# Two heads' scores in neighbouring PSUM banks, and one exponential for both, in a two-layer cross-attention kernel

## The chip, the cores and the metric

The kernel runs as one program on one core of one Trainium2 chip. Its work is spread over five engines: TensorE (PE in the profile, with PEld for its weight loads), VectorE (DVE), ScalarE (ACT), GpSimd (POOL) and SyncE (SP), which issues nearly all DMAs. The metric is the device time of one execution in microseconds, as a median over runs.

## The reference

Two layers, each of a self-attention, a cross-attention and a gated feed-forward part, on four sequences of 512 tokens of width 320, with a context of 1601 tokens of width 192 for each sequence. There are 20 heads of width 16. Everything is float32.

```python
def _attn(x, ctx, wq, wk, wv, wo, bo, heads):
    q, k, v = heads_of(x @ wq), heads_of(ctx @ wk), heads_of(ctx @ wv)
    sim = einsum('bhid,bhjd->bhij', q, k) * dh ** (-0.5)
    out = einsum('bhij,bhjd->bhid', softmax(sim), v)
    return out.transpose(0, 2, 1, 3).reshape(b, n, heads * dh) @ wo + bo

h1 = _ln(x, n1_g, n1_b);  x = _attn(h1, h1, q1, k1, v1, o1_w, o1_b, heads) + x
h2 = _ln(x, n2_g, n2_b);  x = _attn(h2, context, q2, k2, v2, o2_w, o2_b, heads) + x
h3 = _ln(x, n3_g, n3_b);  a, g = split(h3 @ ff_w1 + ff_b1, 2)
x = a * gelu(g) @ ff_w2 + ff_b2 + x
```

(The two layers' code is the same; `heads_of` stands for the reshape and transpose into heads.)

## The kernel before

The work is cut into units. A unit is one layer, one kind (self or cross), one sequence and one group of four heads; a feed-forward unit is one sequence of one layer. There are 20 self units and 20 cross units in each layer. The keys of a unit go in chunks of 128: four chunks in a self unit, 13 in a cross unit (the last has 65 keys), so 680 chunks in all.

For each chunk, `score` makes the scores of one head, transposed (keys on partitions, 512 queries in the columns), in one PSUM bank called "st", by three products of 32 rows each: two for query parts `q` (a value is split into a high and a low part) and one that adds the negative row maximum `nrows`. `exponential` then reads the bank with one ACTIVATE (line 1290) into an SBUF buffer "pr". There are four such buffers to a chunk, one for each head.

Beside the scores of a unit, the row maxima of a later one are made: `max_pairs` (line 1040) makes scores in the other orientation, in banks called "sps", and DVE reduces each bank to a maximum (line 1069), into `pm` for a cross unit and into `nmax` for a self unit. Four heads sit in four row groups of PE, so that a product of each runs at the same time. `round_of` (line 1243) lays the products of a chunk out in slots: heads 0 and 1 of the scores in slots 0 to 2 with "sps" of heads 2 and 3 in slots 0 and 1, then heads 2 and 3 of the scores in slots 2 to 4 with "sps" of heads 0 and 1 in slots 3 and 4. A full chunk thus uses four "st" and four "sps" banks, which are all eight of PSUM.

After the slots of a chunk come the products with the values for the chunk before (`values`, line 1299, put off through `late` and `flush`): eight matmuls into one bank "av", for which a bank must be free. For chunk 0 the bank is copied to `o`; for later ones ACT copies it to a buffer "vo" (line 1325) and POOL adds that to `o` (line 1326). In the last unit ahead of a feed-forward part DVE adds straight from the bank. Then `steps` (line 473) puts in small pieces of other units' work: the projections "qkps" and "qps", the context's keys "kps" (line 951), values "vps" (line 1015), the output projection "ops" (line 1209), and the DMAs that go with them.

The order on every engine is the order in which the program emits the work. Which bank a product gets is decided as the program is written, by a planner: `expect` holds the time at which the program believes each engine to be free, `written` and `busy` move it on by a booked cost, and `bank` gives the bank that will be free first. The same times decide, in `taken` (line 991), whether DVE or ACT copies a small product out of PSUM. Each of the eight banks is a pool slot of its own, and the chip's waits follow from which bank was given.

The buffers "pr", "vo", "gl" (the gate of the feed-forward part, line 1462) and the warm-up operand "fill" come in turn from one pool of nine buffers of 512 columns.

Of the kernel before, what the change touches and what calls it, by code (L numbers as in the profile page):

```python
# [75 lines left out]
def kernel(ctx: ExitStack, tc: tile.TileContext, x, context, ws, out):  # L76
# [27 lines left out]
    prs = ctx.enter_context(tc.tile_pool(name="prs", bufs=9))  # L104
# [27 lines left out]
    fill = prs.tile([P, N], F32, tag="pr", name="fill")  # L132
# [264 lines left out]
    bank_of = {}  # L397

    def bank(name):
        i = min(range(NB), key=lambda i: bank_free[i])  # L400
        assert bank_free[i] < HELD, name
        t = psum.tile([P, 512], F32, tag=f"bank{i}", name=name)
        bank_of[id(t)] = [i, t, bank_free[i], 0.0]
        bank_free[i] = HELD
        return t
# [6 lines left out]
    def busy(engine, us, *tiles):  # L412
        expect[engine] = max([expect[engine]] + [bank_of[id(t)][3] + 0.05 for t in tiles]) + us
        for t in tiles:
            bank_free[bank_of[id(t)][0]] = expect[engine] + 0.09
# [854 lines left out]
    def main(u, give, nxt):  # L1270

        pr, raised = {}, {}

        def score(c, j):
            r = min(P, u.nkeys - c * P)
            rows = slice(j * SLOT, (j + 1) * SLOT)
            own = []

            def product(e):
                nc.tensor.matmul(  # L1280
                    own[0][:r, :],
                    lhsT=ones[rows, :r] if e == 2 else u.keys(rows, c),
                    rhs=u.rows[rows, :] if e == 2 else u.q[rows, e, :],
                    start=(e == 0),
                    stop=(e == 2),
                )

            def exponential():
                p = prs.tile([P, N], F32, tag="pr", name="pr")
                nc.scalar.activation(p[:r], own[0][:r], AF.Exp)  # L1290
                pr[c, j] = p
                busy("act", 0.515, *own)
                raised[c] = expect["act"]

            return (j,), [lambda e=e: product(e) for e in range(3)], exponential, own, lambda: own.append(bank("st"))
# [3 lines left out]
        def values(c):  # L1299
# [18 lines left out]
            if c == 0:  # L1318
                u.o = two.tile([P, N], F32, tag="o", name="o")
                (nc.vector.tensor_copy if last else nc.scalar.copy)(u.o, ps)  # L1320
            elif last:
                nc.vector.tensor_tensor(u.o, ps, u.o, ALU.add)
            else:
                vo = prs.tile([P, N], F32, tag="pr", name="vo")
                nc.scalar.copy(vo, ps)  # L1325
                nc.gpsimd.tensor_tensor(u.o, u.o, vo, ALU.add)  # L1326
# [3 lines left out]
        for c in range(u.nch):  # L1330
            extra = []
            if last:
                round_of([lambda j=j: score(c, j) for j in range(HG)])
                tick()
            else:
                products = []
                for odd in range(2):
                    if odd:
                        tick()
                    pair, rounds = give(2 * c + odd)  # L1340
                    extra += rounds
                    products += [lambda j=j: score(c, j) for j in ((2, 3) if odd else (0, 1))] + pair
                round_of(products)
# [71 lines left out]
    def ff_main(u, give, nxt):  # L1415
# [44 lines left out]
        def gate(c, pss):  # L1460
            gl = prs.tile([P, N], F32, tag="pr", name="gl")
# [5 lines left out]
        def banks():  # L1467
            return [[bank("fps") for _ in range(2)] for _ in range(2)]
# [3 lines left out]
        for j, c in enumerate(ORDER):  # L1472
            ahead = pss is not None
            some = []
            if not ahead:
# [3 lines left out]
                pss = [some, [bank("fps") for _ in range(2)]] if some else banks()  # L1479
# [7 lines left out]
            if not ahead:  # L1487
                rests(c, these, False)
                if j + 1 < len(ORDER):
                    pss = banks()  # L1490
                    rests(ORDER[j + 1], pss, True)
# [237 lines left out]
```

## Time and profile before

| What | Value |
|---|---|
| median of the runs | 3000.01 us |
| lowest and highest of three | 2998.21 and 3005.65 us |
| the profiled execution's own time | 3000.91 us |
| its span, first to last instruction | 2999.1 us |
| TensorE clock granted | 0.993 of full speed |
| exponentials (line 1290) | 2720, of 603 ns in the mean |

The profile names an instruction by its line and by out<-in, with the program's names for tiles. A matmul's end is modelled, so PE's busy share is not a share of its peak. A line of waits says which engine and line waited for which, with the total in microseconds, the number of times and the longest; a wait of PEld is that of a weight load, which stands in front of its matmul. A line of the timeline has the start and length in microseconds, then the instruction, how many of them were merged, and in brackets the engine's idle time before it with what ended it.

The scores of line 1280 run from 44.5 to 2722.2 us, with a pause in the middle (three of 40 equal slices of the span without any) in which the first layer's feed-forward part lies; the second layer's lies behind them.

### The profile page before, as it was taken

The page shows a single profiled execution, that of the slowest core. Times are in us where ns is not written, and L with a number is a line of the kernel's source. Part 1 is how long each engine was busy: PE and PEld are TensorE (multiplying, and loading weights), DVE is VectorE, ACT ScalarE, POOL GpSimd, SP SyncE. Part 2 cuts the span into 40 slices and gives each one's busy share as a digit, 9 for nine tenths or more (in the row PEclk, how much of TensorE's full clock was granted, in tenths as well). Part 3 has the DMA queues.
Part 4 walks back from the last instruction along what each step waited for, and adds up shares of the span by engine and source line. Part 5 has one row for each costly group of instructions (what it writes and reads, how often), then busy time and mean ns, then how long its engine had stood idle before and what let it go on. Part 6 is the DMA issues. An engine that isn't in the chain of part 4 may idle for free.

```text
span 2999.1 us, 84363 instructions
## 1 busy us (share of the span) xinstructions
PE 2885.4 (96%) x35018; PEld 1509.7 (50%) x35018; DVE 2150.8 (72%) x4143; ACT 1892.7 (63%) x3746; POOL 1194.0 (40%) x1305
## 2 busy tenths in 40 slices
PE   8999999999999999999999899999999999999999
PEld 4455554555554554355554555555555555544555
DVE  6877888889889888323268788888888888873221
ACT  3766677877877878501147676778778778784000
POOL 3444344544544545211224443445445454451110
PEclk9999999999999999999999999999999999999999
DMA  4444223132232122200123342222221121222000
GB/s 107 103 122 102 71 74 96 46 90 60 53 82 67 39 56 60 82 17 15 37 60 74 91 99 66 66 58 53 53 64 46 49 70 44 54 54 76 22 22 14
DMA packets 186543, 188.70 MB, mean 63 GB/s; under 512 B 69668, under 2 KB 137264, under 8 KB 186160
## 3 DMA queue, kind: packets, MB, share of 16 engines
q1 hardware_dynamic: 185368, 182.11, 24.0%
q8 instruction: 276, 4.52, 0.6%
q10 hardware_dynamic: 760, 1.18, 0.2%
q14 instruction: 107, 0.88, 0.1%
q0 software_dynamic: 32, 0.00, 0.0%
HBM read 55.76 MB, written 29.36 MB: 28 GB/s over the span
## 4 chain that ended last, share of the span: by engine, by line
PE 77%; DVE 18%; DMA 1%; issue 1%; ACT 1%; POOL 1%; SPq 1%; ACTq 0%; DVEq 0%; POOLq 0%
PE av L1306 21%; PE st L1280 15%; PE fps L1391 9%; DVE pm L1069 9%; PE sps L1054 6%; PE yps L1498 6%; PE vps L1015 4%; DVE nmax L1069 4%; PE ops L1209 3%; PE kps L951 3%; PE qkps L886 3%; PE fps L1451 2%; PE qps L927 2%; PE sps L1081 1%; DVE hturned L608 1%
## 5 line engine op out<-in xcount | busy, mean ns | idle before, releaser
L1290 ACT ACTIVATE pr<-st 128x512 f32<-128x512 f32 (+1 forms) x2720 | 1405.0, 603 | 429.1 <-PE st L1280 381.4
L1069 DVE TENSOR_REDUCE pm<-sps 128x1 f32<-128x512 f32 x1920 | 1185.3, 681 | 129.6 <-PE sps L1054 121.5
L1326 POOL TENSOR_TENSOR o<-o,vo 128x512 f32<-128x512 f32 x576 | 740.7, 1286 | 1125.9 <-ACT vo L1325 1114.3
L1054 PE MATMUL sps<-kT,q 32*128 32x512 f32 x4800 | 874.4, 429 | 13.7 <-DMA q<-low 4.3
L1306 PE MATMUL av<-pr,vals 128*32 128x512 f32 (+1 forms) x5440 | 738.4, 609 | 74.7 <-DVE nmax L1069 19.3
L1280 PE MATMUL st<-q,kT 32*128 32x512 f32 (+1 forms) x5120 | 795.7, 421 | 7.1 <-DVE pm L1069 6.4
L1280 PEld LDWEIGHTS st<-q,kT 32*128 32x128 f32 (+1 forms) x5120 | 422.9, 180 | 299.5 <-issue 120.1
L1280 PE MATMUL st<-nrows,ones 32*128 32x512 f32 (+1 forms) x2720 | 542.6, 399 | 5.4 <-DMA nrows<-turned 5.4
L1054 PEld LDWEIGHTS sps<-kT,q 32*128 32x128 f32 x4800 | 424.0, 183 | 102.2 <-DVE pm L1069 26.8
L1069 DVE TENSOR_REDUCE nmax<-sps 128x1 f32<-128x512 f32 x640 | 395.2, 680 | 81.1 <-PE sps L1054 77.9
L1325 ACT COPY vo<-av 128x512 f32<-128x512 f32 x576 | 352.3, 612 | 26.8 <-PE av L1306 24.7
L1462 ACT ACTIVATE gl<-fps,b 128x512 f32<-128x512 f32 x80 | 54.8, 687 | 414.3 <-PE fps L1451 303.0
L1306 PEld LDWEIGHTS av<-pr,vals 128*32 128x32 f32 (+1 forms) x5440 | 111.1, 108 | 348.8 <-DVE pm L1069 180.7
L1391 PE MATMUL fps<-hT,w 128*128 128x512 f32 x640 | 283.2, 597 | 0.0
L1280 PEld LDWEIGHTS st<-nrows,ones 32*128 32x128 f32 (+1 forms) x2720 | 247.0, 180 | 28.2 <-DMA nrows<-turned 4.8
L1463 DVE SCALAR_TENSOR_TENSOR hid<-fps,b,gl 128x512 f32<-128x512 f32 x80 | 59.7, 748 | 238.8 <-ACT gl L1462 236.7
L1391 PEld LDWEIGHTS fps<-hT,w 128*128 128x128 f32 x640 | 119.2, 190 | 155.1 <-issue 152.6
L1498 PE MATMUL yps<-w,hid 128*128 128x320 f32 x640 | 176.0, 435 | 0.1
L1498 PEld LDWEIGHTS yps<-w,hid 128*128 128x128 f32 x640 | 120.4, 190 | 56.4 <-ACT gl L1462 5.3
L1209 PEld LDWEIGHTS ops<-wo,aT 112*32 112x32 f32 (+1 forms) x3072 | 98.0, 110 | 64.6 <-issue 42.9
L1209 PE MATMUL ops<-wo,aT 112*32 112x160 f32 (+1 forms) x3072 | 126.2, 301 | 0.9 <-DVE pm L1069 0.9
L1505 DVE TENSOR_TENSOR x<-yps,x 128x320 f32<-128x320 f32 x32 | 15.7, 492 | 145.9 <-PE yps L1498 145.9
(89 smaller groups left out, 2476.1 us busy)
## 6 DMA issues: line engine op xcount, KB each, us to landing
kT<-stages SPq DMA_DIRECT2D x160, 200.2 KB
oway<-o SPq DMA_DIRECT2D x80, 256.0 KB
q<-high SPq DMA_DIRECT2D x160, 64.0 KB
q<-low SPq DMA_DIRECT2D x160, 64.0 KB
kT<-high SPq DMA_DIRECT2D x60, 128.0 KB
q<-high SPq DMA_DIRECT2D x60, 128.0 KB
kT<-low SPq DMA_DIRECT2D x57, 128.0 KB
aT<-oway SPq DMA_DIRECT2D x32, 224.0 KB
```

Of the source, the lines that this page charges most:

```text
L886: nc.tensor.matmul(ps[f : f + m, :w], lhsT=wqk[:n, k, f // GD, column : column + m], rhs=first.hT[:n, k, at : at + w], start=(k == 0), sto ...
L1015: nc.tensor.matmul(ps[f : f + m, :w], lhsT=u.kvT[:n, k, at + f : at + f + m], rhs=wv[:n, k, h0 * DH : h1 * DH], start=(k == 0), stop=(k == ...
L1054: nc.tensor.matmul(ps, lhsT=u.q[j * SLOT : (j + 1) * SLOT, e, t * P : (t + 1) * P], rhs=u.kT[j * SLOT : (j + 1) * SLOT, u.k0 + s * 512 : u ...
L1069: nc.vector.tensor_reduce(to[:, j : j + 1], ps, AX.X, ALU.max, negate=(ns == 1))
L1209: nc.tensor.matmul(ps[f : f + m, : D // 2], lhsT=aT[:n, k, f * NQ + t * SLOT : f * NQ + t * SLOT + m], rhs=wo[:n, k, cols], start=(k == 0) ...
L1280: nc.tensor.matmul(own[0][:r, :], lhsT=ones[rows, :r] if e == 2 else u.keys(rows, c), rhs=u.rows[rows, :] if e == 2 else u.q[rows, e, :], ...
L1290: nc.scalar.activation(p[:r], own[0][:r], AF.Exp)
L1306: nc.tensor.matmul(ps[j * SLOT : (j + 1) * SLOT, :], lhsT=columns_of[:r, head : head + SLOT], rhs=pr.pop((c, j))[:r, :], start=True, stop= ...
L1325: nc.scalar.copy(vo, ps)
L1326: nc.gpsimd.tensor_tensor(u.o, u.o, vo, ALU.add)
L1391: nc.tensor.matmul(ps, lhsT=w1[:, k, i * FF + c * P : i * FF + (c + 1) * P], rhs=natural(u.hT[:, k]), start=start, stop=stop,)
L1498: nc.tensor.matmul(ps[:, :D], lhsT=hid[c][:, t * P : (t + 1) * P], rhs=w2[:, c, :], start=(c == 0), stop=(c == NHC - 1),)
```

## The change

`score` now makes the scores of two heads, in two neighbouring banks of which the first has an even number, and one ACTIVATE of 1024 columns reads both into two neighbouring buffers. The order of the products in the slots stays as it was. The eight banks become one PSUM tile of eight slices; `bank` can give two of them at once, and takes for that the even pair whose later one is free first. `busy` marks both banks as read. The planner books 0.88 us for the exponential of two heads, where it booked 0.515 us for one.

The nine buffers become one SBUF tile. Pairs of heads take slices 0 to 7 in turn, two chunks' worth. A "vo" of an odd chunk takes the slice in which head 2 of its own chunk was, which `values` has read by then, and one of an even chunk takes slice 8, as does the warm-up operand. The gate takes all nine in turn. The function `banks` of the feed-forward part is only renamed.

```diff
-    prs = ctx.enter_context(tc.tile_pool(name="prs", bufs=9))
+    prs = ctx.enter_context(tc.tile_pool(name="prs", bufs=1))
...
-    fill = prs.tile([P, N], F32, tag="pr", name="fill")
+    raise_to = prs.tile([P, 9, N], F32, name="pr")
+    raises = {"pair": 0, "sum": 0, "gate": 0}
+
+    def turn_of(what, n):
+        raises[what] += 1
+        return raises[what] % n
+
+    fill = raise_to[:, 8]
...
-    def bank(name):
-        i = min(range(NB), key=lambda i: bank_free[i])
-        assert bank_free[i] < HELD, name
-        t = psum.tile([P, 512], F32, tag=f"bank{i}", name=name)
-        bank_of[id(t)] = [i, t, bank_free[i], 0.0]
-        bank_free[i] = HELD
+    banks = psum.tile([P, NB, 512], F32, name="banks")
+
+    def bank(name, n=1):
+        at = min(range(0, NB - n + 1, n), key=lambda i: max(bank_free[i : i + n]))
+        free = max(bank_free[at : at + n])
+        assert free < HELD, name
+        t = banks[:, at] if n == 1 else banks[:, at : at + n]
+        bank_of[id(t)] = [range(at, at + n), t, free, 0.0]
+        for i in range(at, at + n):
+            bank_free[i] = HELD
         return t
...
         for t in tiles:
-            bank_free[bank_of[id(t)][0]] = expect[engine] + 0.09
+            for i in bank_of[id(t)][0]:
+                bank_free[i] = expect[engine] + 0.09
...
-        def score(c, j):
+        def score(c, heads):
             r = min(P, u.nkeys - c * P)
-            rows = slice(j * SLOT, (j + 1) * SLOT)
             own = []
 
             def product(e):
-                nc.tensor.matmul(
-                    own[0][:r, :],
...
+                for i, j in enumerate(heads):
+                    rows = slice(j * SLOT, (j + 1) * SLOT)
+                    nc.tensor.matmul(
+                        own[0][:r, i],
...
             def exponential():
-                p = prs.tile([P, N], F32, tag="pr", name="pr")
+                at = 2 * turn_of("pair", 4)
+                p = raise_to[:, at : at + 2]
                 nc.scalar.activation(p[:r], own[0][:r], AF.Exp)
-                pr[c, j] = p
-                busy("act", 0.515, *own)
+                for i, j in enumerate(heads):
+                    pr[c, j] = p[:, i]
+                summing[c] = p[:, 0]
+                busy("act", 0.88, *own)
                 raised[c] = expect["act"]
 
-            return (j,), [lambda e=e: product(e) for e in range(3)], exponential, own, lambda: own.append(bank("st"))
+            return heads, [lambda e=e: product(e) for e in range(3)], exponential, own, lambda: own.append(bank("st", 2))
...
-                vo = prs.tile([P, N], F32, tag="pr", name="vo")
+                vo = summing.pop(c) if c % 2 else raise_to[:, 8]
...
-                round_of([lambda j=j: score(c, j) for j in range(HG)])
+                round_of([lambda j=j: score(c, (j, j + 1)) for j in range(0, HG, 2)])
...
-                    products += [lambda j=j: score(c, j) for j in ((2, 3) if odd else (0, 1))] + pair
+                    products += [lambda j=2 * odd: score(c, (j, j + 1))] + pair
...
-            gl = prs.tile([P, N], F32, tag="pr", name="gl")
+            gl = raise_to[:, turn_of("gate", 9)]
```

More of the change, by code (lines that the diff above doesn't have):

```diff
@@ L1465, in gate, with four @@
             busy("dve", 0.66, pss[0])
-        def banks():
+        def four():
             return [[bank("fps") for _ in range(2)] for _ in range(2)]
@@ L1478, in ff_main @@
                 begun.clear()
-                pss = [some, [bank("fps") for _ in range(2)]] if some else banks()
+                pss = [some, [bank("fps") for _ in range(2)]] if some else four()
             for e in range(2):
@@ L1489, in ff_main @@
                 if j + 1 < len(ORDER):
-                    pss = banks()
+                    pss = four()
                     rests(ORDER[j + 1], pss, True)
```

12 lines of the change are left out of this document (6 added, 6 removed).

## The prediction

> **What bounds the kernel now.** I read the page first (busy shares, the chain that ended last), then the groups by line, then the waits, and last the timeline of one chunk of a cross unit.
>
> ```profile
> span 2999.1 us, 84363 instructions
> PE 2885.4 (96%) x35018; PEld 1509.7 (50%) x35018; DVE 2150.8 (72%) x4143; ACT 1892.7 (63%) x3746; POOL 1194.0 (40%) x1305
> PE 77%; DVE 18%; DMA 1%; issue 1%; ACT 1%; POOL 1%; SPq 1%; ACTq 0%; DVEq 0%; POOLq 0%
> PE av L1306 21%; PE st L1280 15%; PE fps L1391 9%; DVE pm L1069 9%; PE sps L1054 6%; PE yps L1498 6%; PE vps L1015 4%; DVE nmax L1069 4%; PE ops L1209 3%; PE kps L951 3%; PE qkps L886 3%; PE fps L1451 2%; PE qps L927 2%; PE sps L1081 1%; DVE hturned L608 1%
> ```
>
> PE is busy for 96% of the span and carries 77% of the chain. DVE carries 18%, and 9% and 4% of that are the row maxima of line 1069. ACT, whose instructions the change merges, is 63% busy and has 1% of the chain. So ACT's throughput is not what is short. The waits say what PE lacks:
>
> ```profile
> ACT pr L1290 <- PE st L1280: 381.4, 510, 23.2
> PEld av L1306 <- DVE pm L1069: 180.7, 354, 1.6
> PEld st L1280 <- ACT pr L1290: 97.5, 134, 0.8
> PEld av L1306 <- ACT pr L1290: 79.1, 160, 0.7
> PEld av L1306 <- DVE nmax L1069: 68.7, 103, 4.7
> PE av L1306 <- DVE nmax L1069: 19.3, 13, 4.2
> ```
>
> The product "av" does not read the maxima of line 1069. It waits for them because it needs a PSUM bank: four score banks and four "sps" banks are all eight, and whichever is read out first is av's. That is a reduction 354 + 103 times and an exponential 160 times. ACT itself waits for PE for 381.4 us, so it has idle time to spare. One chunk:
>
> ```profile
> 803.20 0.49 PE L1280 MATMUL st<-q,kT 32*128 32x512 f32 x2
> ...
> 803.54 0.40 PE L1054 MATMUL sps<-kT,q 32*128 32x512 f32 x2
> ...
> 803.98 2.48 DVE L1069 TENSOR_REDUCE pm<-sps 128x1 f32<-128x512 f32 x4 [0.27 <-PE sps L1054]
> ...
> 804.19 2.06 ACT L1290 ACTIVATE pr<-st 128x512 f32<-128x512 f32 x4 [0.86 <-PE st L1280]
> ...
> 804.24 0.39 PE L1280 MATMUL st<-nrows,ones 32*128 32x512 f32 x2
> ...
> 804.72 0.16 PEld L1306 LDWEIGHTS av<-pr,vals 128*32 128x32 f32 x8 [0.52 <-DVE pm L1069]
> 804.73 1.06 PE L1306 MATMUL av<-pr,vals 128*32 128x512 f32 x8
> ...
> 806.12 0.62 ACT L1325 COPY vo<-av 128x512 f32<-128x512 f32 x1
> 806.40 0.49 PE L1280 MATMUL st<-q,kT 32*128 32x512 f32 x2
> ...
> 806.97 0.39 PE L1280 MATMUL st<-nrows,ones 32*128 32x512 f32 x2
> 806.98 0.40 PE L1280 MATMUL st<-q,kT 32*128 32x512 f32 x2
> ```
>
> The first reduction starts at 803.98, as soon as its scores are there, and with it av's bank comes free; the weights of av start at 804.72. The four exponentials run from 804.19 to 806.25. The chunk starts at 803.20 and the next at 806.40, and its second pair of scores (heads 2 and 3) at 806.98.
>
> **The change, part by part.**
>
> ```profile
> L1290 ACT ACTIVATE pr<-st 128x512 f32<-128x512 f32 x2560 | 1323.3, 603 | 403.8 <-PE st L1280 367.6 <-PE sps L1081 27.2 <-PE sps L1054 4.5
> L1325 ACT COPY vo<-av 128x512 f32<-128x512 f32 x576 | 352.3, 612 | 26.8 <-PE av L1306 24.7 <-POOL root L521 0.6
> L997 ACT COPY vals<-vps 128x192 f32<-128x192 f32 x48 | 15.7, 328 | 20.8 <-PE vps L1015 20.2
> L935 ACT ACTIVATE low<-qps 128x256 f32<-128x256 f32 x40 | 15.4, 385 | 23.9 <-PE qps L927 23.9
> L1290 ACT ACTIVATE pr<-st 65x512 f32<-65x512 f32 x160 | 82.0, 594 | 25.3 <-PE st L1280 13.8 <-PE sps L1054 11.3
> L1069 DVE TENSOR_REDUCE pm<-sps 128x1 f32<-128x512 f32 x1920 | 1185.3, 681 | 129.6 <-PE sps L1054 121.5 <-PE st L1280 3.5
> ```
>
> *The exponential.* 2560 + 160 instructions of 512 columns become 1360 of 1024. No row shows 1024 columns. From 256 to 512 columns an ACTIVATE goes from 385 to 603 ns, 0.85 ns a column; copies of 192 and 512 columns give 0.89. So 512 more columns cost 436 ns (to 454), and the long one takes 1.04 us. Four exponentials took 2.06 us in the chunk, so they start (2.06 - 0.60) / 3 = 0.49 us apart; two of 1024 start 0.49 + 0.43 = 0.92 apart. A pair saves 2 x 0.49 - 0.92 = 0.05 us, about 70 us of ACT over 1360. I cost this gain at nothing: ACT's 381.4 us of waiting for PE cover it.
>
> *When banks come free.* In the chunk shown, the first score bank is free at 804.19 + 0.60 = 804.79 now and the other three by 806.25. After the change the first two are free together at 805.23 and the last two at 806.15: the first bank comes 0.44 us later, the last 0.10 earlier. Where a reduction gives av its bank, nothing moves: it ends about 804.67, ahead of both. Where an exponential does (160 waits), av waits longer, by 0.44 us at most and by nothing where a reduction ends just then. The rows do not say which; I take half, 0.22 x 160 = +35 us (ends 0 and 70).
> The Trainium skill speaks against the change here: Perfetto Trace Analysis, section Optimizing Scalar/DVE Operations, says that where Scalar or Vector is not saturated but causes bubbles on other engines, breaking instructions up may let work finish sooner. This trace agrees as far as ACT at 63% ends 160 waits of av; by that rule taken in full the term is its upper end, 70 in place of 35, and the sum is 35 us higher.
>
> *Two neighbouring banks.* A pair of scores now needs an even bank and the next one both free, while sps, av and the copied products take the single bank that is free first and so break pairs. By hand from the chunk: av takes the bank of the first reduction, the next small product one of heads 0 and 1; the next chunk's first pair takes two banks free by 806.15, and its second pair is left with av's bank and that of the last reduction. The last reduction ends at 803.98 + 2.48 = 806.46, the copy of av, which starts 0.11 before the exponential ahead of it ends (0.60 - 0.49), at 806.15 - 0.11 + 0.61 = 806.65. The pair is wanted at 806.98, so 0.33 us is spare, and the steady chunk loses nothing. Chunks where scores wait for exponentials already (134 waits) can lose up to 0.44 each: 0 to 59 us; I take a quarter, +15, since the chunk shown has slack.
>
> *The buffer of vo.* In odd chunks vo now lies in the buffer of heads 2 and 3 of its own chunk, which the second exponential of the chunk after next writes again; before, the buffer came back one chunk later.
>
> ```profile
> L1326 POOL TENSOR_TENSOR o<-o,vo 128x512 f32<-128x512 f32 x576 | 740.7, 1286 | 1125.9 <-ACT vo L1325 1114.3 <-DMA w<-in_L_xattn_ff_w_dram 4.0 <-DMA nrows<-turned 2.7
> L804 POOL TENSOR_TENSOR stages<-stages 128x801 f32<-128x801 f32 x40 | 64.1, 1603 | 3.2
> L803 POOL CAST stages<-stages 128x801 fp32r<-128x801 f32 x40 | 34.2, 856 | 43.3 <-ACT stages L997 16.6 <-DVE stages L994 10.9 <-DVE pm L1069 8.7
> ```
>
> POOL's addition would end at 806.65 + 1.29 = 807.94, and that exponential starts one chunk (803.20 to 806.40, 3.20 us) after 805.11, at 808.31: 0.37 us spare. The 40 splits of 0.86 + 1.60 us on POOL's queue can push an addition past that, in half the chunks: 20 x (2.46 - 0.37) = 42 us of late exponentials at most. Behind a waiting exponential stand the vo copy and ACT's evictions, and behind those PE's banks; ACT's idle time takes most of it. +5 us.
>
> *Copies that change engine.* The planner gives a small copy to the engine it believes free first, and it now books 0.88 us a pair in place of 1.03, so some go from DVE to ACT.
>
> ```profile
> L994 DVE COPY vals<-vps 128x192 f32<-128x192 f32 (+3 forms) x167 | 53.3, 320 | 39.2 <-PE vps L1015 33.6 <-POOL o L1326 1.7
> L994 DVE COPY stages<-kps 128x200 f32<-128x200 f32 (+1 forms) x120 | 44.2, 369 | 40.8 <-PE kps L951 25.9 <-ACT vo L1325 4.0 <-issue 3.1
> ```
>
> DVE does 287 of them, 98 us. Fewer can only help where DVE is behind. The waits for pm are 180.7 / 354 = 0.51 us, the 0.52 of the chunk shown, whose reduction began at once, so there is no backlog to win. The waits for nmax are 68.7 / 103 = 0.67, so 0.15 x 103 + 19.3 = 35 us is the most. I take -10 (ends -35 and 0).
>
> The slices that stand for tiles (first warm-up operand, gate buffers) add no work.
>
> **Sum.** 35 + 15 + 5 - 10 = +45 us (ends -35 and +171). The profiled execution took 3000.91 us, 1.8 more than its span; 3046 by it, and 3045 by the median of the runs, 3000.01, which is 0.9 below it. The runs lie within 0.25% of each other, so about 0.3% (9 us) is what can be told from no change.
>
> **The rivals.**
> *Faster:* ACT's room takes the copies off DVE, and the planner, which books the score banks later, hands av a reduction's bank each time. The wait is av behind nmax and the 160 behind exponentials lose nothing: -35 us, less the 5 for vo, 2970. For it: DVE's 18% of the chain. Against: the pm waits hold no backlog. It decides where the 160 waits cost under 0.1 us each. 0.22.
> *Nothing measurable:* a reduction frees av's bank in nearly all chunks and the slack of 0.33 us holds for the pairs: 3000. For it: 457 of the 617 waits of av. 0.10.
> *Broken pairs cost every chunk:* the second pair waits for the last reduction or the copy of av. It begins when DVE is over 0.5 us late or ACT 0.33. At 0.25 us over the 520 chunks of the cross units (two layers of 20 units of 13) it is +130, 3131. For it: DVE at 72% over all, with copies ahead of reductions. Against: the slack. 0.14.
> *Shared tiles are waited for whole,* so that the change does not do what it says: av waits for the latest exponential, 806.15 in place of 804.67, 1.48 us in 680 chunks (1360 pairs), about 4000 us. Against it:
>
> ```profile
>   DVE pm L1069: 190.7, 367
>   ACT pr L1290: 95.1, 230
>   DVE nmax L1069: 88.0, 116
>   issue: 12.5, 32
>   DVE pm L1091: 2.5, 7
>   DVE turned L1123: 1.4, 3
>   DVE parts L1119: 0.4, 1
> ```
>
> This is all that av's line waits for, and the copies into "vals", one tile that av reads while later chunks are copied into it, are not there. But no PSUM tile is shared yet. 0.04.
>
> **How the numbers follow.** The forecast, slower by 45 us, has 0.50, its own range 3015 to 3085. With the rivals: slower 0.50 + 0.14 + 0.04 = 0.68, same 0.10, faster 0.22. The range for 8 in 10 takes in most of the faster case and the lower half of the broken pairs: 2970 to 3115.
>
> **What would show it.** Exponentials: 1360 of about 1.04 us, some 70 us less ACT busy. The waits of av for pr: fewer or as many, but longer on the mean than 0.49 us. The waits of st for pr or for pm: longer. Copies of line 994: fewer than 287. POOL as a releaser of the exponentials: new, a few us. The prediction is wrong if av's waits for pr all but vanish while those for pm stay, or if PE waits for pairs in most chunks.

## The result and the profile after

The changed kernel takes 3027.37 us in the median (3027.20 to 3030.76), the kernel before 3001.51 over the runs made beside it: a ratio of 1.0088, with a 95% interval from 1.0075 to 1.0101. It is slower by 26 us, on the side that was forecast and inside the range, at about 0.6 of the 45 us. The profiled execution of after took 3027.30 us, its span is 3025.5, and its granted clock is 0.993, as in before.

In after every PSUM tile is called "banks" and every exponential's buffer "pr", so its products must be told apart by line: 1292 makes the scores for the exponentials ("st" before), 1065 and 1092 those for the maxima ("sps"), 1321 is the product with the values ("av"), 1080 the reductions, 1303 the exponential, 1340 the copy of av and 1341 the addition on POOL.

The page of after, busy shares and the chain by engine:

```profile
span 3025.5 us, 84304 instructions
PE 2875.7 (95%) x35018; PEld 1518.0 (50%) x35018; DVE 2157.9 (71%) x4153; ACT 1825.6 (60%) x2376; POOL 1194.1 (39%) x1305
...
PE 76%; DVE 17%; issue 2%; ACT 2%; POOL 1%; DMA 1%; SPq 1%; DVEq 0%; POOLq 0%; ACTq 0%
```

ACT is busy for 67.1 us less (1892.7 before) and the kernel is slower all the same. ACT's share of the chain has gone from 1% to 2%. The groups that carry the change, from the page of after (the last number of the middle part is the mean time of one in ns):

```profile
L1303 ACT ACTIVATE pr<-banks 128x1024 f32<-128x1024 f32 (+1 forms) x1360 | 1329.7, 1022 | 460.5 <-PE banks L1292 395.3
...
L1292 PEld LDWEIGHTS banks<-q,kT 32*128 32x128 f32 (+1 forms) x5120 | 434.3, 180 | 315.5 <-ACT pr L1303 131.9
...
L1321 PEld LDWEIGHTS banks<-pr,vals 128*32 128x32 f32 (+1 forms) x5440 | 108.1, 108 | 392.1 <-DVE pm L1080 227.7
```

and the two lines of weight loads that answer to them, from the page of before:

```profile
L1280 PEld LDWEIGHTS st<-q,kT 32*128 32x128 f32 (+1 forms) x5120 | 422.9, 180 | 299.5 <-issue 120.1
...
L1306 PEld LDWEIGHTS av<-pr,vals 128*32 128x32 f32 (+1 forms) x5440 | 111.1, 108 | 348.8 <-DVE pm L1069 180.7
```

The weight loads of av stand idle 43.3 us longer, those of the scores 16.0 longer. A wait of a weight load can lie beside matmuls that still run, so these are no losses as they stand; the starts of the matmuls, below, say what was lost. The releasers, some rows from the waits of after:

```profile
ACT pr L1303 <- PE banks L1292: 395.3, 566, 4.9
PEld banks L1321 <- DVE pm L1080: 227.7, 409, 1.6
PEld banks L1292 <- ACT pr L1303: 133.8, 212, 1.7
PEld banks L1321 <- DVE nmax L1080: 92.0, 130, 3.8
PEld banks L1321 <- ACT pr L1303: 45.2, 50, 1.1
PE banks L1321 <- DVE pm L1080: 38.8, 102, 1.2
PE banks L1321 <- DVE nmax L1080: 33.9, 51, 3.4
ACT pr L1303 <- POOL o L1341: 15.0, 51, 0.7
```

Av was released by an exponential 160 times and is now 50 times, at 45.2 / 50 = 0.90 us each where it was 0.49. A reduction releases it oftener (409 + 130 against 354 + 103 times), and that is where the waiting grew: for pm from 180.7 to 227.7 us and for nmax from 68.7 to 92.0, while the waits for exponentials fell from 79.1 to 45.2. One and the same chunk, where both changes are seen, first in the timeline of before:

```profile
685.91 2.06 ACT L1290 ACTIVATE pr<-st 128x512 f32<-128x512 f32 x4 [0.66 <-PE st L1280]
...
685.96 0.39 PE L1280 MATMUL st<-nrows,ones 32*128 32x512 f32 x2
...
686.56 1.07 PE L1306 MATMUL av<-pr,vals 128*32 128x512 f32 x8 [0.21 <-ACT pr L1290]
...
687.03 2.44 DVE L1069 TENSOR_REDUCE pm<-sps 128x1 f32<-128x512 f32 x4
687.73 0.50 PEld L951 LDWEIGHTS kps<-ctxT,w 96*32 96x32 f32 x16 [1.02 <-DVE pm L1069]
687.73 0.89 PE L951 MATMUL kps<-ctxT,w 96*32 96x200 f32 x16
...
688.55 0.45 PE L1280 MATMUL st<-q,kT 32*65 32x512 f32 x2
```

and then in that of after:

```profile
695.75 1.94 ACT L1303 ACTIVATE pr<-banks 128x1024 f32<-128x1024 f32 x2 [0.78 <-PE banks L1292]
...
695.78 0.39 PE L1065 MATMUL banks<-kT,q 32*128 32x512 f32 x1
...
696.81 2.44 DVE L1080 TENSOR_REDUCE pm<-banks 128x1 f32<-128x512 f32 x4
...
696.83 1.07 PE L1321 MATMUL banks<-pr,vals 128*32 128x512 f32 x8 [0.65 <-ACT pr L1303]
...
697.71 0.86 PE L962 MATMUL banks<-ctxT,w 96*32 96x200 f32 x16
...
698.50 0.44 PE L1292 MATMUL banks<-q,kT 32*65 32x512 f32 x2
```

Before, an exponential of 0.60 us that began at 685.91 let av start at 686.56; the product after it then waited for a reduction and started 1.17 us after av. After, the exponential that began at 695.75 lets av start at 696.83, 1.08 us behind it in place of 0.65; the product after it finds its bank free and starts 0.88 us after av. Most of what av loses here, the next product gives back: from the exponential's start to that product it is 687.73 - 685.91 = 1.82 us before and 697.71 - 695.75 = 1.96 after.

To see this for the whole span, I added up the time from the start of each matmul to the start of the next, over all of PE's matmuls of a profiled execution, and sorted it into four: from a score product to a score product right behind it; from a chunk's last score product to av; from av's first product until the first product behind av; and everything else. A score product is here one of either kind, for the exponentials or for the maxima.

| us of the profiled span | among the scores | scores to av | av to the next | other | span |
|---|---|---|---|---|---|
| before | 856.1 | 318.0 | 649.4 | 1170.2 | 2999.1 |
| after | 857.3 | 363.0 | 630.0 | 1170.0 | 3025.5 |
| difference | +1.2 | +45.0 | -19.4 | -0.2 | +26.4 |

(The span also holds 5.3 us ahead of the first matmul and behind the last one's start, the same in both.) So the whole loss lies ahead of av, 45 us, and 19 of it come back behind av. The experiments show that the +1.2 among the scores is not "nothing", but a sum of larger terms of opposite signs.

### The profile page after: what moved, and what is told of

The parts are those of the page before. It is cut to its first block, busy times and chain, and to the rows that moved or that the text cites. A ratio compares the mean times of both kernels' runs of the same rounds, so it can differ in the third digit from the quotient of the medians.

```text
span 3025.5 us, 84304 instructions
## 1 busy us (share of the span) xinstructions
PE 2875.7 (95%) x35018; PEld 1518.0 (50%) x35018; DVE 2157.9 (71%) x4153; ACT 1825.6 (60%) x2376; POOL 1194.1 (39%) x1305
## 4 chain that ended last, share of the span: by engine, by line
PE 76%; DVE 17%; issue 2%; ACT 2%; POOL 1%; DMA 1%; SPq 1%; DVEq 0%; POOLq 0%; ACTq 0%
PE banks L1321 21%; PE banks L1292 15%; DVE pm L1080 10%; PE banks L1406 9%; PE banks L1513 6%; PE banks L1065 5%; PE banks L1026 5%; PE banks L1220 3%; DVE nmax L1080 3%; PE banks L962 3%; PE banks L897 3%; PE banks L1466 2%; PE banks L938 2%; ACT pr L1303 2%; PE banks L1092 1%
## 5 line engine op out<-in xcount | busy, mean ns | idle before, releaser
L1303 ACT ACTIVATE pr<-banks 128x1024 f32<-128x1024 f32 (+1 forms) x1360 | 1329.7, 1022 | 460.5 <-PE banks L1292 395.3
L1080 DVE TENSOR_REDUCE pm<-banks 128x1 f32<-128x512 f32 x1920 | 1187.5, 682 | 132.0 <-PE banks L1065 122.6
L1341 POOL TENSOR_TENSOR o<-o,pr 128x512 f32<-128x512 f32 x576 | 741.4, 1287 | 1151.2 <-ACT pr L1340 1124.6
L1065 PE MATMUL banks<-kT,q 32*128 32x512 f32 x4800 | 862.4, 428 | 11.2 <-DMA q<-high 3.0
L1321 PE MATMUL banks<-pr,vals 128*32 128x512 f32 (+1 forms) x5440 | 732.6, 608 | 116.9 <-DVE pm L1080 38.8
L1292 PE MATMUL banks<-q,kT 32*128 32x512 f32 (+1 forms) x5120 | 816.1, 422 | 10.7 <-DVE pm L1080 2.9
L1292 PEld LDWEIGHTS banks<-q,kT 32*128 32x128 f32 (+1 forms) x5120 | 434.3, 180 | 315.5 <-ACT pr L1303 131.9
L1292 PE MATMUL banks<-nrows,ones 32*128 32x512 f32 (+1 forms) x2720 | 556.7, 395 | 1.2 <-DMA nrows<-turned 1.2
L1065 PEld LDWEIGHTS banks<-kT,q 32*128 32x128 f32 x4800 | 427.2, 183 | 78.8 <-ACT pr L1303 17.2
L1080 DVE TENSOR_REDUCE nmax<-banks 128x1 f32<-128x512 f32 x640 | 396.2, 681 | 81.9 <-PE banks L1065 79.4
L1321 PEld LDWEIGHTS banks<-pr,vals 128*32 128x32 f32 (+1 forms) x5440 | 108.1, 108 | 392.1 <-DVE pm L1080 227.7
```

Of the source, the lines that this page charges most:

```text
L1065: nc.tensor.matmul(ps, lhsT=u.q[j * SLOT : (j + 1) * SLOT, e, t * P : (t + 1) * P], rhs=u.kT[j * SLOT : (j + 1) * SLOT, u.k0 + s * 512 : u ...
L1080: nc.vector.tensor_reduce(to[:, j : j + 1], ps, AX.X, ALU.max, negate=(ns == 1))
L1292: nc.tensor.matmul(own[0][:r, i], lhsT=ones[rows, :r] if e == 2 else u.keys(rows, c), rhs=u.rows[rows, :] if e == 2 else u.q[rows, e, :], ...
L1321: nc.tensor.matmul(ps[j * SLOT : (j + 1) * SLOT, :], lhsT=columns_of[:r, head : head + SLOT], rhs=pr.pop((c, j))[:r, :], start=True, stop= ...
```

## The experiments

One execution can lie 8 us off its kernel's median: of the kernel below that splits only the first pair, the profiled one took 3026.60 us at a granted clock of 0.990, and two at 0.993 took 3018.04 and 3018.34. Costs are therefore taken from the medians, and the sums of starts are read for the place.

**Sharing the tiles, with single exponentials.** First both shared tiles alone: before, with the eight banks as slices of one PSUM tile and the nine buffers as slices of one SBUF tile, in the same turn as before.

```diff
-        t = psum.tile([P, 512], F32, tag=f"bank{i}", name=name)
+        t = banks[:, i]
...
-                p = prs.tile([P, N], F32, tag="pr", name="pr")
+                p = in_turn()
```

> The kernel before, with the eight banks as slices of one PSUM tile and the nine buffers as slices of one SBUF tile; one exponential a head, single banks, the buffers in turn. Theory (the loss of 26 us is the later release of the first score bank): as before, 3001 us within 6, av waiting for the exponentials about 160 times as before. Rival (sharing one tile brings waits of its own): 3015 to 3030 us, and av waiting longer for the reductions of the maxima.

Measured: 3013.52 us against 3001.69, ratio 1.0046 (1.0030 to 1.0061), between the two times that were expected. To tell the two tiles apart, only the banks:

```diff
-        t = psum.tile([P, 512], F32, tag=f"bank{i}", name=name)
+        t = banks[:, i]
```

> The kernel before with the eight banks as slices of one PSUM tile and nothing else; the nine buffers come from their pool as before. With both tiles shared it was 1.0046. If the PSUM tile brings that cost: 3009 to 3017 us, and ACT's and DVE's queues hold more semaphore instructions than before. If the buffers bring it: 2997 to 3006 us.

Measured: 3002.67 us against 3000.44, ratio 1.0006 (0.9997 to 1.0015). So the one PSUM tile costs nothing that can be told from no change, and what the first kernel loses comes with the one SBUF tile, or with the two tiles together (the SBUF tile alone was not run). Its trace shows a difference on ACT's queue. These are the semaphore instructions at the exponential's line, for before, both tiles, banks only and after, in this order (the number behind the first x counts them):

```profile
L1290 ACTq EVENT_SEMAPHORE  x483: 17/17/17, 57.2 to 2722.9; - x161
```

```profile
L1299 ACTq EVENT_SEMAPHORE  x2709: 17/17/4198, 60.6 to 2735.4; - x194
```

```profile
L1292 ACTq EVENT_SEMAPHORE  x641: 17/17/4197, 59.3 to 2721.4; - x161
```

```profile
L1303 ACTq EVENT_SEMAPHORE  x492: 17/17/19093, 56.8 to 2749.3; - x164
```

With nine slices in turn, nearly each of the 2720 exponentials has such an instruction ahead of it, and an exponential that ACT was idle for starts 87 ns after the end of the last score product ahead of it, where it is 29 in before (medians, worked out from the starts and the modelled ends in the trace). After has 492 of them and 37 ns, so this cost is not in the changed kernel.

Then the changed kernel's own tiles and its own turn of buffers, but with single banks and two exponentials (the edit without its branch, which is always taken here):

```diff
-                nc.scalar.activation(p[:r], own[0][:r], AF.Exp)
+                for i in range(2):
+                    nc.scalar.activation(p[:r, i], own[i][:r], AF.Exp)
+                    busy("act", 0.515, own[i])
...
-... lambda: own.append(bank("st", 2))
+... lambda: own.extend([bank("st"), bank("st")])
```

> The changed kernel's shared tiles and its turn of buffers, with two single banks, wherever they are free, and two exponentials of 512 columns for each two heads. It differs from the run with two exponentials to a pair (1.0123) only in that the banks need not be neighbours. Theory now (the need for an even pair costs some 25 us): 3005 to 3016 us. Rival (sharing the tiles or the buffers' turn costs it): 3030 to 3040 us.

Measured: 3020.71 us against 3000.88, ratio 1.0060 (1.0048 to 1.0073), again between the two times that were expected. Some of this may be clock: its run with a granted clock of 0.991 took 3013.84 us, and the runs of before on that chip at 0.991 took 3000.23 and 3002.36, so 11 to 14 us are there at the same clock, and the rest of the 20 goes with runs at 0.989 and 0.990. That the first kernel's cost isn't clock is seen in the same way: its two runs at 0.993 took 3010.26 and 3013.66, and before at 0.992 to 0.994 took 2997.75 to 3004.47. The semaphore instructions are few in it (717), and its exponentials start 28 ns behind their scores, as in before. One part has a row, in what its exponentials waited for; no exponential waited for that addition in before:

```profile
  POOL o L1347: 18.7, 52
```

This is the buffer of vo, to which an experiment below gives 4 us by the medians, and more at the same clock. What the rest is made of was not found.

**Pairs of banks, and which of the two exponentials is the long one.** Four kernels make a square: the changed one, and three in which heads 0 and 1, heads 2 and 3, or both have two exponentials of 512 columns, each of which frees its own bank of the pair:

```diff
-                nc.scalar.activation(p[:r], own[0][:r], AF.Exp)
+                if heads[0] == 0:          # or == 2, or True
+                    at, free = bank_of[id(own[0])][0], bank_of[id(own[0])][3]
+                    for i in range(2):
+                        nc.scalar.activation(p[:r, i], own[0][:r, i], AF.Exp)
+                        expect["act"] = max(expect["act"], free + 0.05) + 0.515
+                        bank_free[at[i]] = expect["act"] + 0.09
+                else:
+                    nc.scalar.activation(p[:r], own[0][:r], AF.Exp)
+                    busy("act", 0.88, *own)
-                busy("act", 0.88, *own)
```

Both pairs with two exponentials:

> The changed kernel, with two exponentials of 512 columns for each pair of banks, each of which gives its own bank free; the even pairs, the shared tiles and the buffers stay. Theory (late release): the first score bank comes free early again, 3000 to 3010 us. Rival (the even pairs cost, since a pair needs both banks free): 3020 to 3035 us, with scores waiting inside the chunk.

Only the first pair (heads 0 and 1) with two:

> The changed kernel, with two exponentials of 512 columns for heads 0 and 1 and one of 1024 for heads 2 and 3. Theory (what costs is the release of the first bank of a chunk, 0.42 us later): most of the loss goes, 3000 to 3012 us, and av's waits are back at the 103 us of before. Rival (every long exponential costs, or the pairs do): half of the loss or all of it, 3013 to 3027 us.

Only the second pair with two:

> The mirror of the run with heads 0 and 1 split: one exponential of 1024 columns for heads 0 and 1, two of 512 for heads 2 and 3. Theory (release of the first bank): the loss stays, 3020 to 3030 us. Rival (every long exponential costs alike): 3010 to 3016 us.

Measured, each beside 3001.69 of before (after beside 3001.51):

| median, us (ratio, interval) | second pair: two of 512 | second pair: one of 1024 |
|---|---|---|
| first pair: two of 512 | 3038.58 (1.0123, 1.0109 to 1.0136) | 3018.78 (1.0065, 1.0051 to 1.0078) |
| first pair: one of 1024 | 3048.58 (1.0161, 1.0147 to 1.0176) | 3027.37 (1.0088, 1.0075 to 1.0101) |

The kernel with two and two, and the one with only the second pair split, lie above every time that was expected of them; the one with only the first pair split lies where its rival put it. The two merges act each by itself. Merging the first pair costs 10.0 us (3048.58 - 3038.58) or 8.6 (3027.37 - 3018.78); merging the second gains 19.8 (3038.58 - 3018.78) or 21.2. Pairs of banks without a long exponential cost 18 us against the kernel with single banks and the same tiles (3038.58 - 3020.71), or 25 against its run at 0.991 (3013.84; the kernel with two and two ran at 0.992 and 0.993). Where these lie, in the sums of starts:

| us of the profiled span | among the scores | scores to av | av to the next |
|---|---|---|---|
| single banks, two exponentials (same tiles) | 865.7 | 318.0 | 655.9 |
| pairs, two and two | 910.1 | 311.2 | 642.5 |
| pairs, two and one long | 881.9 | 317.3 | 644.7 |
| pairs, one long and two | 885.9 | 355.4 | 632.8 |
| pairs, both long (after) | 857.3 | 363.0 | 630.0 |

Three effects can be read off by rows that differ in one edit. Pairs of banks put 44 us among the scores, and take 7 away ahead of av and 13 behind it. The long exponential of the first pair puts 44 to 46 us ahead of av, and takes 24 to 25 away among the scores and 10 to 15 behind av, 34 to 39 in all. The long exponential of the second pair takes 28 away among the scores and puts 6 to 8 ahead of av. The group of the scores' weight loads shows the same, in the kernel with two and two:

```profile
L1292 PEld LDWEIGHTS banks<-q,kT 32*128 32x128 f32 (+1 forms) x5120 | 439.5, 180 | 352.1 <-ACT pr L1306 130.1 <-issue 105.7 <-DVE pm L1080 40.4
```

Its idle time of 352.1 us was 299.5 in before and is 315.5 in after. And the first merge's own wait, in the kernel where only the first pair is split:

```profile
L1328 PEld LDWEIGHTS banks<-pr,vals 128*32 128x32 f32 (+1 forms) x5440 | 108.4, 108 | 346.4 <-DVE pm L1080 186.8 <-DVE nmax L1080 74.0 <-ACT pr L1306 52.7
```

346.4 us of idle time ahead of av's loads is again that of before (348.8), against 392.1 in after. So the 45 us ahead of av come with the merge of the first pair, but undoing it gains 9 us only, since the products among the scores then take 25 more and those behind av 15.

What the second merge shortens is less clear. If its gain came from banks that the exponentials free earlier, the scores should wait less for exponentials. Their waits with only the first pair split, and then with only the second:

```profile
PEld banks L1292 <- ACT pr L1306: 82.9, 104, 0.8
...
PEld banks L1292 <- ACT pr L1310: 60.9, 141, 1.6
```

```profile
PEld banks L1292 <- ACT pr L1306: 104.4, 178, 0.8
...
PEld banks L1292 <- ACT pr L1310: 23.8, 34, 0.8
```

That is 143.8 us with the second pair merged, against 134.4 with two and two, and 133.8 in after against 128.2: not shorter. Shorter are their loads' waits for the reductions of pm, from 39.7 to 25.8 us where the first pair is one, and hardly where it is two (41.6 to 40.3). An edit that splits a pair also changes what the planner books, 1.03 us in place of 0.88, and with it which banks are given; the booking is tried alone below.

The Trainium skill, Perfetto Trace Analysis, section Optimizing Scalar/DVE Operations, says that where Scalar is not saturated but causes bubbles, breaking up instructions may let work finish sooner. The square agrees for the exponential whose banks av waits for (9 to 10 us) and not for the one behind it, where breaking up costs 20.

**The first pair apart.** Heads 0 and 1 take two single banks and two exponentials, heads 2 and 3 keep the pair and the long one, so that only the long exponential that gains needs neighbouring banks.

```diff
+            apart = heads[0] == 0
...
-... lambda: own.append(bank("st", 2))
+... lambda: own.extend([bank("st"), bank("st")] if apart else [bank("st", 2)])
```

> Heads 0 and 1 in two single banks with two exponentials of 512 columns, heads 2 and 3 in an even pair with one of 1024; all else as in the changed kernel. Theory now (the long exponential of the second pair gives 20 us back, that of the first costs 9, the pairs cost 25 together): 2990 to 3008 us. Rival (a pair costs as much where only one is asked for): 3015 to 3022 us, as where both are pairs and the first has two exponentials.

Measured: 3130.32 us against 3000.88, ratio 1.0426 (1.0411 to 1.0440): a clear miss. Among the scores it takes 1008.0 us, 152 more than before. From its waits (line 1293 makes the scores):

```profile
PEld banks L1293 <- DVE pm L1080: 150.9, 190, 2.3
...
PE banks L1293 <- DVE pm L1080: 63.6, 92, 1.8
```

and from those of before:

```profile
PEld st L1280 <- DVE pm L1069: 49.1, 112, 2.0
...
PE st L1280 <- DVE pm L1069: 6.4, 8, 1.1
```

Scores wait for reductions now, 214.5 us in place of 55.5. Sorted by the place of the product in its chunk, 155 of these 214.5 us stand ahead of the first products of heads 2 and 3. So two single banks, given by whichever is free first, break pairs, and the pair for heads 2 and 3 then needs a bank that a reduction still reads. This is the third rival of the prediction, "broken pairs cost every chunk", in a kernel where it does hold; measured are 129 us over before. (That the rival was priced at 130 is chance, since its 0.25 us a chunk was a point picked on a scale.) The granted clock of its runs is 0.984 to 0.987, which may be part of the loss.

**A bank picked so as to spare whole pairs.** Where several single banks are free by the time PE gets there, the one whose neighbour is free last is taken.

```diff
+        if n == 1:
+            at = min(range(NB), key=lambda i: (max(bank_free[i], expect["pe"]), -bank_free[i ^ 1]))
```

> The changed kernel, in which a single bank is taken, among those that are free by then in the plan, from the pair whose other bank is in use longest, so that whole pairs are spared. Theory (scores wait for a whole pair, and av for a bank that comes 0.42 us later; the two take each other's place): the waits inside the chunk fall, av's stay, 3015 to 3027 us. Rival (broken pairs are the larger part): 3000 to 3014 us.

Measured: 3036.11 us against 3000.44, ratio 1.0128 (1.0111 to 1.0144), worse than after and than either time that was expected. Against after the sums have +23.9 among the scores (881.2), -20.3 ahead of av (342.7) and +0.4 behind it; the runs that make the median have after's clock. Av finds its bank sooner and the scores find theirs later: they wait for exponentials 294 times, 212 in after. Why the exchange is a loss was not settled.

**The booking.** The planner books 1.03 us for a long exponential, what it booked for two before, and not 0.88.

```diff
-                busy("act", 0.88, *own)
+                busy("act", 1.03, *own)
```

> The changed kernel with 1.03 us in place of 0.88 booked for a long exponential: no instruction is longer, only the planner's choice of banks and of the copies' engine moves. Theory (what the second long exponential gave back is the real end of the pair, 0.1 us earlier): within 8 us of the changed kernel, 3019 to 3035 us. Rival (it came from the booking, by which banks are chosen otherwise): 3040 to 3050 us.

Measured: 3035.79 us, ratio 1.0113 (1.0099 to 1.0126): 8 us more than after by the medians, of which some may be clock (all its runs are at 0.990; after's one run at 0.991 took 3030.76, 4 to 6 us less). It lies just above what was expected if the second merge's gain is the real end of its pair, and below what was expected if it is the booking: the booking, here changed for both pairs, can hold a part of the 20 us, and not most of them. The loss lies ahead of av (374.8 us, 11.8 more). The small copies that DVE does rise from 297 to 314 of 432, so the lower booking does send copies to ACT, as the prediction had it. Whether these 17 copies or the other choice of banks make the difference was not separated.

**The buffer of vo.** Every vo in slice 8.

```diff
-                vo = summing.pop(c) if c % 2 else raise_to[:, 8]
+                vo = raise_to[:, 8]
```

> The changed kernel with every vo in slice 8, so that no exponential waits for POOL; the vo copy then waits for the addition of the chunk before. Theory (the buffer of vo costs little): 3022 to 3030 us, with POOL gone from what the exponentials wait for. Rival (vo in a head's buffer is a good part of the loss): 3005 to 3015 us.

Measured: 3023.32 us, ratio 1.0069 (1.0055 to 1.0083), 4 us under after by the medians, with intervals that overlap. At the same clock it is more: its runs at 0.991 took 3023.32 to 3024.22 and after's 3030.76, at 0.993 it is 3019.64 against 3027.30 and 3030.06, and at 0.994 3016.63 against 3027.28, so 7 to 11 us. The row of after in which exponentials wait for POOL's addition (15.0 us, 51 times) is gone from its waits, so the buffer did what was said, at a price of 4 to 11 us.

**All small copies on ACT.** This tests the prediction's claim that DVE holds no backlog to win. In before:

```diff
-        if expect["dve"] < expect["act"]:
+        if False:
```

> The kernel before, with every small copy out of PSUM on ACT, where the planner gave 287 of 432 to DVE. If DVE's backlog stands behind av's waits, they fall and the time is 2970 to 2995 us. If av waits for reductions that begin at once (as the prediction read the 0.51 us), it is 2995 to 3020 us, since ACT's copies now stand in front of its exponentials.

Measured: 2990.36 us against 3000.44, ratio 0.9970 (0.9959 to 0.9982). This beats both kernels. Its page:

```profile
span 2988.4 us, 84215 instructions
PE 2873.4 (96%) x35018; PEld 1515.4 (51%) x35018; DVE 2059.1 (69%) x3856; ACT 1959.2 (66%) x4033; POOL 1194.5 (40%) x1305
...
L1069 DVE TENSOR_REDUCE pm<-sps 128x1 f32<-128x512 f32 x1920 | 1187.7, 681 | 235.5 <-PE sps L1054 224.2
...
L1306 PEld LDWEIGHTS av<-pr,vals 128*32 128x32 f32 (+1 forms) x5440 | 111.0, 108 | 364.9 <-DVE pm L1069 221.8
```

The reductions' idle time ahead of them goes from 129.6 us (page of before) to 235.5: with 287 copies fewer DVE is there ahead of its scores far oftener, so before it was not. (The planner's times move with the copies, and so does its choice of banks; what each of the two is worth was not separated.) The wait of av doesn't show the gain, it even grows (348.8 to 364.9). The gain lies in the other two stretches: among the scores 843.8 us (-12.3), behind av 635.3 (-14.1), against +15.6 ahead of av.

The same edit in the changed kernel:

> The changed kernel, with every small copy out of PSUM on ACT. The prediction's faster rival had ACT's room take the copies off DVE: then 2985 to 3015 us, at least 10 us under the changed kernel, and more is won than in the kernel before. If ACT's room is worth nothing: 3020 to 3045 us.

Measured: 3012.74 us against 3000.44, ratio 1.0040 (1.0026 to 1.0054), 15 us under after, mostly among the scores (837.1, -20.2). So the room that the long exponentials make on ACT is worth about 5 us more for copies than in before (15 against 10), within what two such differences can be told apart, and not enough: with all copies on ACT in both, the change still costs 3012.74 - 2990.36 = 22 us.

## Why the prediction was right, and where its sum was not

**The bound.** ACT is busy for 67 us less (forecast 70), with 1.02 us an instruction (forecast 1.04), and the kernel is slower: its throughput is not what was short.

**The late first release, +35 (0 to 70).** The place was right, and the size there near: +45.0 us ahead of av, which splitting the first pair takes away again. That the size is so near is in part luck: the step priced longer waits for exponentials in 160 places, and av's loads wait less for exponentials in all (45.2 us, 79.1 before) and more for the reductions whose banks they get in their place. What the step left out is the other side of av's wait. The work behind av waited for reductions that run on meanwhile, so 34 to 39 us of the 45 come back among the scores and behind av, and the first merge costs 9 to 10 net. The chunk at 685.91 shows it: in before a wait of 1.02 us for a reduction stands right behind av, and in after it is gone. The prediction priced a wait by its own length and did not ask what is late next.

**Two neighbouring banks, +15 (0 to 59).** Right in kind and near in size: 18 us by the medians (25 against the single-bank kernel's run at 0.991). The place was right too: in the kernel with pairs and no long exponential the scores wait for exponentials 252 times, 134 in before. These are more waits and not longer ones, 134.4 us in all against 97.5, where the prediction had the 134 grow (the row of the waits):

```profile
PEld banks L1292 <- ACT pr L1306: 134.4, 252, 0.8
```

In after itself the term can't be read off the stretch among the scores, which grew by 1.2 us, because the long exponentials take 24 and 28 away there.

**"The last 0.10 earlier", priced at nothing.** This is the largest thing that the sum left out. The prediction worked out both sides of the merge (the first bank 0.44 us later, the last two 0.10 earlier) and priced the first alone. Merging the second pair's exponentials gains 20 us, and the square shows this with either form of the first. The cause stays open. That the gain comes from two banks which are free together and earlier, when the next chunk's pairs want both, is argued and not shown: the four heads' exponentials end 0.12 us earlier in the chunks above (1.94 in place of 2.06), and 0.12 over the 520 chunks of the cross units, 62 us, would hold it, but the scores' waits for exponentials did not shorten with the second merge. The lower booking can hold a part.

**The buffer of vo, +5 (0 to 42).** 4 us by the medians of its experiment, 7 to 11 at the same clock, and the releaser that was forecast is there: 51 waits of 15.0 us in all.

**Copies that change engine, -10 (-35 to 0).** The copies went the other way. From the groups of after, by line:

```profile
L1005 DVE COPY vals<-banks 128x192 f32<-128x192 f32 (+3 forms) x176 | 56.8, 323 | 47.8 <-PE banks L1026 36.8 <-POOL o L1341 1.7 <-ACT hT L640 0.9
...
L1005 DVE COPY stages<-banks 128x200 f32<-128x200 f32 (+1 forms) x121 | 44.6, 368 | 43.0 <-PE banks L962 16.6 <-ACT pr L1303 9.9 <-ACT pr L1340 7.3
```

DVE does 176 + 121 = 297, not fewer than 287. The booked 0.88 does move copies to ACT (314 with 1.03), but against before the count did not fall, so the term, as forecast, was 0. And "the pm waits hold no backlog to win" does not hold for the kernel as a whole: all copies off DVE gained 10 us in before, at a place that av's waits don't show.

**Shared tiles.** They are not waited for whole: one PSUM tile costs nothing that can be told (1.0006). The sum had no term for them, though, but for the buffer of vo: the changed kernel's tiles and turn of buffers cost 11 to 20 us before any pair is made, of which that buffer is 4 to 11, and the rest has no cause that was shown.

**The sum.** By medians: tiles and buffers +20 (vo in them), pairs +18, first merge +10 or +9, second merge -20 or -21: +27. These steps lead from one kernel to the next, so that they add up to the measured 26 says nothing by itself. The prediction had +5, +15, +35 and nothing, and -10 for the copies: +45. So the sign came out right, and the 18 us too many are the first merge without what came back and the second merge without its gain (25 and 21 too many), less the tiles' cost that was left out and the gain by the copies that did not come (15 and 10 too few), and less 3 for the pairs. That the total came so near is luck in good part, since errors of 10 to 25 us took each other away.

**The rivals.** *Faster* falls: av is released by reductions oftener, as it said (539 against 457), but by longer waits, and DVE did not get the copies off. Where the copies do leave DVE, time is gained: 0.9970 in the kernel before. *Nothing measurable* falls with 1.0088. *Broken pairs cost every chunk* is not what happens in after; it is what happens when two single banks stand ahead of a pair (1.0426).

## What to carry to other kernels

Where PE waits for PSUM banks, price a release by what stands behind the waiting product too: of 45 us that av lost, 34 to 39 came back beside it. Merging two readers into one is not good or bad as such: here it cost 9 us for the banks that were wanted first and gained 20 for the later ones, so try each of them alone. And an engine at 72% with short waits shown against it can still hold the others back: moving its small copies to the engine at 63% gained 10 us, where the merge lost 26.

## What the runs showed of the hardware

One ACTIVATE over two neighbouring banks takes 1022 ns in the mean (1024 in the median), against 603 ns for one bank. Back to back, single ones overlap by 114 ns and the long ones by about 104 (worked out from the starts and ends of neighbours in the traces). The Trainium skill, ScalarE: Activation LUTs, section What ACT_TABLE_LOAD costs, gives 186 ns and 0.833 ns a column for an ACTIVATE with immediate scale and bias, by which 1024 columns would be an estimated 1039, and an overlap of about 93; the measured values are 2% below and some 10 to 20 ns above.

With slices of one SBUF tile given out in turn, and slices of one PSUM tile, this kernel had 2709 semaphore instructions of 17 ns on ACT's queue at the exponential's line, where tiles of their own had 483, and exponentials started 58 ns later behind their scores (87 against 29). Slices of one PSUM tile alone did not (641), nor did the changed kernel's nine slices with a turn of their own (492).

The granted clock is not the same for kernels of the same work: 0.990 to 0.995 in before and 0.991 to 0.994 in after, 0.989 to 0.991 in the kernel with the same tiles and single banks, 0.984 to 0.987 in the one with the first pair apart. Of one and the same kernel, the one split in the first pair, two runs at 0.990 took 3026.60 and 3023.74 us and three at 0.993 took 3017.99 to 3018.34, 5 to 9 us less, so a few thousandths of clock are as much as some of the effects here.
